# Third layer of a four-layer image kernel: token statistics of the mixers from their modes, synthesis blocks summed straight from PSUM, a part of the last stage on Pool

## The chip, the cores and the metric

The kernel runs on one core of a Trainium2 chip. The metric is the device time of one execution in microseconds (us); the time before is the median of three runs. The engines carry their names in the profile: PE (TensorE, the matmuls), PEld (its weight loads), DVE (VectorE), ACT (ScalarE), POOL (GpSimd, called Pool here) and SP (SyncE, which issues most DMAs). Matmuls write to PSUM, from which DVE and ACT read; all other tiles lie in SBUF.

## The reference

Four layers, each a residual step `x = x + layer(groupnorm(x))`, act on `x` of shape [4, 64, 64, 128]: a selective scan, a Fourier layer with feed-forward, an operator attention, and a 7x7 neighbourhood attention. The third layer is the one that changes. It reads `x` as [images, tokens, height, width]: 64 tokens an image, each a plane of 64x128. Its tail, cut to what matters here:

```python
attn = fno_layer(attn, proj_w, proj_skip_w, proj_skip_b, (H, W))
attn = instance_norm(attn + tokens, attn_norm_g, attn_norm_b)
m = instance_norm(attn, norm2_g, norm2_b)
m = fno_layer(m, mixer_w1, ..., norm=(mixer_norm_g1, mixer_norm_b1), act=_gelu)
m = fno_layer(m, mixer_w2, ..., norm=(mixer_norm_g2, mixer_norm_b2))
out = instance_norm(m, mixer_out_g, mixer_out_b) + attn

def fno_layer(x, spec_w, skip_w, skip_b, out_shape, norm=None, act=None):
    xs = conv1x1(x, skip_w, skip_b)          # a scale and a shift here
    xf = spectral_conv(x, spec_w, out_shape) # 32 x 17 modes of the 2D transform, times weights, back
    if norm is not None:
        xf = instance_norm(xf, *norm)        # mean and variance of each token's plane
    y = xf + xs
    return act(y) if act is not None else y
```

A mixer is thus: transform a plane, multiply the low modes by weights, transform back to `xf`, normalize `xf` by its mean and variance over the plane, add the scaled input. All is float32.

## The kernel before, in words

The layers run one after the other on the one core, from about 0 to 5750 us, to 6220, from 6227 to 7208, and to the end. The third layer keeps an image as a tile of 128 partitions by 32 rows by 128 elements (2 MB): a token's plane lies over the 64 partitions of one half and the 128 elements, two tokens to a row, so `m[:, j, :]` belongs to two tokens and a token's mean and variance are a [128, 32] tile with one column for each `j`. `C4` names four chunks of eight `j`.

`layer2_image` (from L1190) is a generator for one image. `Pace.in_turn` (L1163) runs two of them together, images 0 and 1 and then 2 and 3, and always goes on with the one whose next work starts earliest by a table of costs per engine (`spend`, L1129); with `nc.aside` a piece of work does not move its generator's time. The order that comes out is the order of the instructions on PE, ACT, DVE and Pool (`manual_schedule`); SyncE's queue is ordered by the scheduler. All instructions of this layer are recorded through `Pace`, so the profile puts them on one line, L1155, and they are told apart by their tiles. Each engine takes its instructions in this order, so an instruction that waits holds all behind it.

The parts that matter, for a pair of images:

- **`dft_y`** (L1266): eight groups of four matmuls `pu<-an,z` (or `m`), each copied by ACT into `U`.
- **`spectral`** (L1607): after `dft_y`, four quarters of `pq<-U,quad` (PE) times the weights `mix` on DVE into `Zp`, 68 partitions by 64 tokens by 32 modes. Then `synthesis` (L1283): for each of four `g0`, two matmul groups `pa` copied by ACT to `S`, then two blocks `pb` (u = 0 and 1; each four `j`, 128x512). Each block is copied by ACT to the image tile `sp`, and DVE takes `bn_stats` of each of its four rows.
- **`token_stats`** (L1213): small matmuls `in_pm` that add these statistics over the partitions of a token, with a DVE part `in_d` between.
- After the first mixer: the norm's scale `q1` and shift `f1` (ACT square root, small DVE operations); `sp` is scaled and shifted, in chunks 0 and 2 by ACT (`affine`) and in 1 and 3 by DVE, added to `m`, and ACT takes Gelu of each chunk of `m` (L1663).
- After the second: `m = sp*q2 + m`, 32 DVE operations an image, with `bn_stats` (L1688), then `q3`, `f3`, and the last stage: `m*q3+f3` on ACT, `+z` on DVE, chunk 3 all on DVE, and a DMA for each chunk to the output (L1699).
- Beside the first mixer Pool computes **`residual`** (L1642), `z = z*sa + za + xr`, three operations of 128x1024 for each of the four chunks, where `xr` is the image of `x` loaded again; beside the second, **`grown`** (L1678), `m = m*scal(10)`, four operations. They are called from `copied` (L1627), one step after each block; a step of `residual` is two chunks, one of `grown` is one.

Tiles of 2 MB come from the pool `big`, seven buffers in use in turn: `xg`, `ti`, `z`, `U2`, `sp`, `m`, `xr` of both images share them, so a load waits until the buffer's last reader is done. `S` has three buffers, the PSUM tags `a` and `b` three banks each; `held` gives two more for `in_pm`.

The fourth layer starts from the third's output in DRAM: its loads `x<-x` follow the last output DMAs on SyncE.

Of the kernel before, what the change touches and what calls it, by code (L numbers as in the profile page):

```python
# [11 lines left out]
F32 = mybir.dt.float32  # L12
AF = mybir.ActivationFunctionType
# [4 lines left out]
P = 128  # L18
# [986 lines left out]
def layer2_weights(sh, A, wp, setup, ps, wt, w):  # L1005
# [18 lines left out]
    for n in (1, 2):  # L1024
        load(f"mix{n}", [Q, 32], A[f"mix{n}"])
    pa, pb, vra, vrb, via, vib = (load(name, [Q, 32, 16], A[name], setup) for name in ("pa", "pb", "vra", "vrb", "via", "vib"))
# [22 lines left out]
    for n in (1, 2):  # L1049
        m = w[f"mix{n}"]  # L1050
        nc.vector.tensor_scalar(m, m, qc[:, 0:1], None, ALU.mult)
# [138 lines left out]
def layer2_image(sh, w, pools, x_in, x_out, scr, wt, parity, beside):  # L1190
# [75 lines left out]
    def dft_y(src, scale=None, then=None):  # L1266

        U = large("U2", [P, 2, 32, 64])
        for g in range(NJ // 4):
# [5 lines left out]
            if scale is None:  # L1275
                nc.scalar.copy(Ug, pg)
            else:
                nc.scalar.activation(Ug, pg, AF.Copy, scale=scale)
                then(g)
# [327 lines left out]
    def spectral(src, mix, beside=()):  # L1607
        beside = iter(beside)
        U = yield from dft_y(src)
        Zm = own([Q, 64, 32], "Zp", tmp)  # L1610
        for g in range(4):
            px = ps.tile([Q, 32, 16], F32, name="pq", tag="b")
            for q in range(2):
                nc.tensor.matmul(
                    px, lhsT=w["quad"][:, q, :], rhs=U[:, q, :, 16 * g : 16 * g + 16], start=(q == 0), stop=(q == 1)
                )
            tt(
                Zm[:, 16 * g : 16 * g + 16, :],
                px.rearrange("p r t -> p t r"),
                mix.unsqueeze(1).to_broadcast([Q, 16, 32]),  # L1620
                ALU.mult,
            )
            yield g == 3
        sp = large("sp")
        st = own([P, NJ, 6], "in_st")

        def copied(u, g0, p):  # L1627
            nc.scalar.copy(at(sp, u, g0), p)
            counted(st, sp, block(u, g0))
            nc.aside = True  # L1630
            next(beside, None)
            nc.aside = False

        yield from synthesis(Zm, copied)
        return sp, st


    m = large("m")
    for c in range(4):
        by_rows(m, z, A2, c, ALU.mult)  # L1640
    yield False
    def residual():  # L1642
        xr = large("xr")
        load_image(nc, xr, x_in)
        for n, c in enumerate(C4):
# [3 lines left out]
            if n % 2:  # L1649
                yield  # L1650

    sp, st = yield from spectral(z, w["mix1"], residual())
    mu, var = yield from token_stats(sp, st)
# [9 lines left out]
    for c in range(5):  # L1663
        if c < 4:
            if c % 2:
                by_rows(m, m, f1, c, ALU.add)
                by_rows(sp, sp, q1, c, ALU.mult)
            else:
                affine(sp, sp, q1, f1, c)
            mc = m[:, C4[c], :]  # L1670
            tt(mc, mc, sp[:, C4[c], :], ALU.add)
        if c > 0:
            mc = m[:, C4[c - 1], :]
            nc.scalar.activation(mc, mc, AF.Gelu)
        yield c == 4


    def grown():  # L1678
        for n, c in enumerate(C4):
            nc.gpsimd.tensor_scalar(m[:, c, :], m[:, c, :], scal(10), None, ALU.mult)  # L1680
            yield

    sp, st = yield from spectral(m, w["mix2"], grown())
    mu, var = yield from token_stats(sp, st)
# [3 lines left out]
    for n in range(4):  # L1688
        js = range(8 * n, 8 * n + 8)
        for j in js:  # L1690
            stt(m[:, j, :], sp[:, j, :], q2[:, j : j + 1], m[:, j, :], ALU.mult, ALU.add)
        counted(st, m, js)
        yield n == 3
# [4 lines left out]
    yield True  # L1698
    for n, c in enumerate(C4):  # L1699
        rows = slice(1024 * n, 1024 * n + 1024)  # L1700
# [482 lines left out]
```

## Time and profile before

| what | us |
|---|---|
| median of three runs | 7777.08 (7775.43 to 7779.66) |
| the profiled execution, its own time | 7781.59 |
| its span in the profile | 7779.7 |
| busy in the span: PE, DVE, ACT, POOL | 6337.0, 6747.1, 6112.9, 5675.9 |
| third layer | 6227 to 7208 |
| tail of its first pair (from the first mixer's transform) | 6520 to 6723 |
| tail of its second pair | 7006 to 7208 |
| last `bn_stats` of the first pair's sum ends | 6702.06 |
| DVE's last operation of the first and second pair ends | 6722.5, 7207.6 |
| first load `x<-x` of the fourth layer issued | 7211.14 |

The profiled execution is 4.5 us above the median. The mean granted TensorE clock over the span is 0.964 of full speed. In the page's rows of 40 slices each digit is the busy share of a slice in tenths (9 is 90% or more). A row of the timeline has the start, the length, the engine, the line, the operation, the tiles (out<-in) with partitions x elements, a count, and in brackets how long the engine had been idle and what released it. A row of a group has busy time and mean ns of one after the bar, and then the idle time before them.

### The profile page before, as it was taken

What the parts mean: (1) busy time and instruction counts of PE and PEld (TensorE: products, weight loads), DVE (VectorE), ACT (ScalarE), POOL (GpSimd) and SP (SyncE); (2) the same over time, 40 slices, a digit from 0 to 9 for tenths busy, and PEclk for the clock granted to TensorE, in tenths of its full rate; (3) what the DMA queues carried; (4) which work ended last, traced back from release to release, by engine and by line L of the source; (5) the groups of instructions that cost most, each with busy time, mean ns of one, the idle gap of its engine ahead of it and who ended that gap; (6) DMA issues with size and microseconds to landing.
All of it is one profiled execution on the core that took longest, in us unless ns stands there. A gap on an engine that the chain in (4) does not pass through costs nothing. (4 is left out here: it accounts for less than half of the span.)

```text
span 7779.7 us, 141035 instructions
## 1 busy us (share of the span) xinstructions
PE 6337.0 (81%) x52796; PEld 3998.2 (51%) x52796; DVE 6747.1 (87%) x8097; ACT 6112.9 (79%) x9715; POOL 5675.9 (73%) x2590
## 2 busy tenths in 40 slices
PE   7888888878889877888887777787779968687789
PEld 3544444444455444445554444444457756564566
DVE  7999999999999999999999999999966646556678
ACT  7999999989999998999999999999843323314667
POOL 4989999988999998999999999999930023223233
PEclk8999999999999999999999999999999978788899
DMA  6555556545565554555655445455532142231332
GB/s 171 173 163 175 174 173 176 170 169 165 186 183 179 185 177 162 163 177 179 180 184 180 168 156 185 160 188 177 181 107 63 43 128 61 71 108 40 103 95 81
DMA packets 1325855, 1158.87 MB, mean 149 GB/s; under 512 B 694133, under 2 KB 1119697, under 8 KB 1258226
## 3 DMA queue, kind: packets, MB, share of 16 engines
q1 hardware_dynamic: 1323010, 1148.47, 48.0%
q8 instruction: 416, 6.82, 0.4%
q14 instruction: 269, 2.20, 0.1%
q10 hardware_dynamic: 2160, 1.38, 0.1%
HBM read 956.37 MB, written 189.21 MB: 147 GB/s over the span
## 5 line engine op out<-in xcount | busy, mean ns | idle before, releaser
L688 DVE TENSOR_TENSOR_SCAN h<-dA,state,dB 128x512 f32<-128x512 f32 x4096 | 4921.0, 1266 | 204.4 <-POOL dB L682 79.5
L682 POOL TENSOR_TENSOR dB<-du,Bb 128x1024 f32<-128x1024 f32 x2048 | 4811.7, 2385 | 342.9 <-DVE h L688 208.6
L538 PE MATMUL pt<-ident,h 128*128 128x128 f32 x16384 | 2221.0, 279 | 875.7 <-ACT hT L548 860.0
L687 ACT ACTIVATE dA<-delta,A_neg 128x512 f32<-128x512 f32 x4096 | 2761.1, 697 | 157.6 <-DVE h L688 129.7
L538 PEld LDWEIGHTS pt<-ident,h 128*128 128x128 f32 x16384 | 1807.0, 142 | 1926.3 <-ACT hT L548 1704.7
L548 ACT COPY hT<-pt 128x1024 f32<-128x1024 f32 x2048 | 2080.2, 1016 | 164.7 <-PE pt L538 146.4
L573 PE MATMUL yT<-hT,W 128*32 128x256 f32 x16384 | 1379.6, 409 | 0.4
L573 PEld LDWEIGHTS yT<-hT,W 128*32 128x32 f32 x16384 | 456.0, 150 | 342.5 <-issue 330.9
L161 PE MATMUL cv<-xn,taps 128*128 128x512 f32 x936 | 527.0, 644 | 2.8 <-DVE delta L474 2.8
L1155 POOL TENSOR_TENSOR xg<-xg,so 128x1024 f32<-128x1024 f32 x16 | 39.3, 2466 | 636.5 <-PE pu L1155 613.6
L1900 POOL TENSOR_TENSOR S<-S,sm 128x784 f32<-128x784 f32 x128 | 191.1, 1493 | 419.1 <-DVE sm L1898 256.3
L477 POOL TENSOR_TENSOR du<-delta,u 128x1024 f32<-128x1024 f32 x128 | 304.3, 2377 | 79.0 <-DVE delta L474 78.9
L465 PE MATMUL dp<-xd,w_dt 65*128 65x512 f32 x512 | 288.8, 646 | 69.9 <-ACT Ct L456 47.0
L448 PE MATMUL xd_ps<-u,w_x 128*48 128x512 f32 x512 | 251.8, 615 | 23.6 <-DVE e L360 18.1
L1907 ACT ACTIVATE S<-S,mx 128x196 f32<-128x196 f32 x512 | 227.8, 448 | 35.9 <-DVE mx L1934 35.4
L161 PEld LDWEIGHTS cv<-xn,taps 128*128 128x128 f32 x936 | 139.2, 188 | 180.5 <-issue 160.4
L914 ACT ACTIVATE h<-pf,b 128x512 f32<-128x512 f32 x128 | 87.7, 687 | 117.2 <-PE pf L913 99.2
L474 DVE SCALAR_TENSOR_TENSOR delta<-delta,dp 128x512 f32<-128x512 f32 x256 | 170.6, 667 | 4.3 <-ACT delta L471 1.0
L1862 PE MATMUL pt<-ident,S 128*98 128x128 f32 x1024 | 166.3, 287 | 3.5 <-POOL S L1900 2.0
L465 PEld LDWEIGHTS dp<-xd,w_dt 65*128 65x128 f32 x512 | 76.5, 188 | 174.5 <-ACT Ct L456 99.9
L1155 POOL TENSOR_TENSOR WX<-wr,Xs 128x544 f32<-128x544 f32 x40 | 58.0, 1449 | 148.2 <-issue 61.8
L471 ACT ACTIVATE delta<-delta 128x512 f32<-128x512 f32 x256 | 165.9, 649 | 0.0
(378 smaller groups left out, 7030.6 us busy)
## 6 DMA issues: line engine op xcount, KB each, us to landing
Bb<-l_B SPq DMA_DIRECT2D x512, 1024.0 KB
W<-l_W SPq DMA_DIRECT2D x512, 256.0 KB
l_y<-y SPq DMA_DIRECT2D x127, 512.0 KB
u<-l_xr SPq DMA_DIRECT2D x64, 512.0 KB
u<-l_xw SPq DMA_DIRECT2D x64, 512.0 KB
y<-l_y SPq DMA_DIRECT2D x56, 512.0 KB
V<-l_v SPq DMA_DIRECT2D x512, 49.0 KB
y<-l_y SPq DMA_DIRECT2D x80, 256.0 KB
```

The costliest lines, as they stand in the source:

```text
L161: nc.tensor.matmul(pm, lhsT=taps[:, s, t, :], rhs=xn[:, dy : dy + 8, dx : dx + 64], start=(t == 0), stop=(t == 8),)
L448: nc.tensor.matmul(bank["x"], lhsT=w_x[:, s, k, :], rhs=u[:, s, :], start=(s == 0), stop=(s == 1))
L465: nc.tensor.matmul(bank[s], lhsT=w_dt[:, k, s * P : (s + 1) * P], rhs=xd, start=True, stop=True)
L477: nc.gpsimd.tensor_tensor(du, delta, u, ALU.mult)
L538: nc.tensor.transpose(pt[:, j, s, :], G["h"][:, s, t0 : t0 + 32, :].rearrange("p t n -> p (t n)"), sh.ident)
L548: return lambda: nc.scalar.copy(hT, pt.rearrange("p j s d -> p j (s d)"))
L573: nc.tensor.matmul(U["yT"][e][32 * jo : 32 * jo + 32, qo % 2, :], lhsT=U["Ws"][G["g"]][:, :, 4 * q + j], rhs=hT[:, j, :], start=((e, jo) n ...
L682: nc.gpsimd.tensor_tensor(dB, du, B_now[:, q : q + 1, :].to_broadcast([P, 2, CH]), ALU.mult)
L687: nc.scalar.activation(dA, delta[:, s, :], AF.Exp, scale=A_neg[:, k, s, n : n + 1])
L688: nc.vector.tensor_tensor_scan(h[:, s, :, q], dA, dB[:, s, :], state[:, s, n : n + 1], ALU.mult, ALU.add)
L1900: nc.gpsimd.tensor_tensor(Sv, Sv, U["sm"].unsqueeze(2).to_broadcast([P, 4, 196]), ALU.mult)
L1907: nc.scalar.activation(Sn, Sn, AF.Exp, bias=U["mx"][:, n : n + 1], accum_out=sm[:, n : n + 1])
```

## The change: what it does

The mixers no longer write the synthesized plane to `sp`. In `spectral`, after each quarter's product `Zp = pq*mix`, a matmul `pn` with a constant matrix `power` (34 x 512) forms sums of the modes' real and imaginary parts, ACT squares it to `sq`, and DVE reduces it over the modes (`tensor_reduce` of modes 1 to 31, `tensor_copy` of mode 0) into `total`. Three small matmuls for each half of the partitions then give a token's mean (from its zeroth mode) and variance (from the sums of squares) in `pm`. For this the weights `mix` are formed in the weights' setup with two more constants (`mir`, `once`), loaded by four more small DMAs.

Because mean and variance are known before the synthesis, `q1` and `f1` are too: `m += f1` by eight rows at a time on DVE, and each block `pb` goes straight from PSUM into the sum, `m = pb*q1 + m` (DVE, one operation for each `j`), with Gelu of a chunk after its last block. `residual` is called from there. In the second mixer the blocks with u = 0 are summed in the same way; those with u = 1 are scaled by ACT into a tile `qs` and added by DVE in one operation; `bn_stats` of the sum follows. `grown` is called from the groups of the second mixer's `dft_y`. In the last stage chunk 0 is computed by Pool (three operations), chunks 1 and 2 as before, chunk 3 on DVE as before.

```diff
--- before
+++ after
@@ layer2_weights
         load(f"mix{n}", [Q, 32], A[f"mix{n}"])
+        load(f"mir{n}", [Q, 32], A[f"mir{n}"], setup)
+    load("power", [Q, 226], A["c_power"])
+    once = load("once", [Q, 32], A["c_once"], setup)
...
-        nc.vector.tensor_scalar(m, m, qc[:, 0:1], None, ALU.mult)
+        nc.vector.scalar_tensor_tensor(m, m, qc[:, 0:1], once, ALU.mult, ALU.mult)
+        nc.vector.scalar_tensor_tensor(m, w[f"mir{n}"], qc[:, 7:8], m, ALU.mult, ALU.add)
@@ layer2_image
-    def spectral(src, mix, beside=()):
-        beside = iter(beside)
-        U = yield from dft_y(src)
+    def spectral(src, mix, then=None):
+        U = yield from dft_y(src, None, then)
         Zm = own([Q, 64, 32], "Zp", tmp)
+        total = own([P, NJ, 6], "in_st")[0:34].rearrange("p j k -> p (j k)")[:, 0:128].rearrange("p (n t) -> p n t", n=2)
         for g in range(4):
+            part = slice(16 * g, 16 * g + 16)
             px = ps.tile([Q, 32, 16], F32, name="pq", tag="b")
             for q in range(2):
+                nc.tensor.matmul(px, lhsT=w["quad"][:, q, :], rhs=U[:, q, :, part], start=(q == 0), stop=(q == 1))
+            tt(Zm[:, part, :], px.rearrange("p r t -> p t r"), mix.unsqueeze(1).to_broadcast([Q, 16, 32]), ALU.mult)
+            yield False
+            pn = ps.tile([34, 16, 32], F32, name="pn", tag="a")
+            nc.tensor.matmul(pn, lhsT=w["power"][:, 0:34], rhs=Zm[:, part, :], start=True, stop=True)
+            sq = tmp.tile([34, 16, 32], F32, name="sq", tag="S2", bufs=3)
+            nc.scalar.activation(sq, pn, AF.Square)
+            nc.vector.tensor_reduce(total[:, 0, part], sq[:, :, 1:32], AX.X, ALU.add)
+            nc.vector.tensor_copy(total[:, 1, part], sq[:, :, 0])
+            yield g == 3
+        pm = held([P, 2, NJ], "in_pm")
+        for u in range(2):
+            half = slice(64 * u, 64 * u + 64)
+            nc.tensor.matmul(pm[half, 0, :], lhsT=w["power"][:, 162:226], rhs=Zm[:, u:64:2, 0], start=True, stop=True)
+            for n in range(2):
                 nc.tensor.matmul(
+                    pm[half, 1, :],
+                    lhsT=w["power"][0:34, 34 + 64 * n : 98 + 64 * n],
+                    rhs=total[:, n, u:64:2],
...
-        sp = large("sp")
-        st = own([P, NJ, 6], "in_st")
-        def copied(u, g0, p):
-            nc.scalar.copy(at(sp, u, g0), p)
-            counted(st, sp, block(u, g0))
...
-    for c in range(5):
-        if c < 4:
-            if c % 2:
-                by_rows(m, m, f1, c, ALU.add)
-                by_rows(sp, sp, q1, c, ALU.mult)
-            else:
-                affine(sp, sp, q1, f1, c)
-            mc = m[:, C4[c], :]
-            tt(mc, mc, sp[:, C4[c], :], ALU.add)
...
+    for c in range(4):
+        if c in (0, 1, 2, 3):
+            by_rows(m, m, f1, c, ALU.add)
...
+    def mixed(u, g0, p):
+        for n, j in enumerate(block(u, g0)):
+            stt(m[:, j, :], p[:, n, :], q1[:, j : j + 1], m[:, j, :], ALU.mult, ALU.add)
+        if u == 1:
+            mc = m[:, C4[g0 // 4], :]
             nc.scalar.activation(mc, mc, AF.Gelu)
+            if (0, 0, 0, 0)[g0 // 4] == 0:
+                aside(rest)
+    yield from synthesis(Zm, mixed)
+    def grown(g):
+        if g % 2:
+            nc.aside = True
+            mc = m[:, C4[g // 2], :]
+            nc.gpsimd.tensor_scalar(mc, mc, scal(10), None, ALU.mult)
+            nc.aside = False
+    Zm, mu, var = yield from spectral(m, w["mix2"], grown)
...
+    def summed(u, g0, p):
+        if u in (1,):
+            t = tmp.tile([P, 4, DM], F32, name="qs", tag="S2", bufs=3)
+            for n, j in enumerate(block(u, g0)):
+                nc.scalar.activation(t[:, n, :], p[:, n, :], AF.Copy, scale=q2[:, j : j + 1])
+            tt(at(m, u, g0), at(m, u, g0), t, ALU.add)
+        for n, j in enumerate(block(u, g0) if u not in (1,) else ()):
+            stt(m[:, j, :], p[:, n, :], q2[:, j : j + 1], m[:, j, :], ALU.mult, ALU.add)
+        counted(st, m, block(u, g0))
...
+    for n in (0,):
+        c = C4[n]
+        nc.aside = True
+        for v, op in ((wide(q3, c), ALU.mult), (wide(f3, c), ALU.add), (z[:, c, :], ALU.add)):
+            nc.gpsimd.tensor_tensor(m[:, c, :], m[:, c, :], v, op)
+        nc.aside = False
+        put(n)
     for n, c in enumerate(C4):
+        if n in (0,):
+            continue
+        if n in (3,):
```

## The prediction

> **What bounds the kernel now.** I read the page's head first, then the table of busy time by stage, then the groups and waits of the stage that the diff touches, then its timeline. From the page, the span and the rows of busy tenths and clock tenths:
>
> ```profile
> span 7779.7 us, 141035 instructions
> PE   7888888878889877888887777787779968687789
> DVE  7999999999999999999999999999966646556678
> ACT  7999999989999998999999999999843323314667
> POOL 4989999988999998999999999999930023223233
> PEclk8999999999999999999999999999999978788899
> ```
>
> Each digit is 194.5 us. Up to digit 29 VectorE is full (the scan). The third layer is digits 33 to 37: there no engine is full. It runs from 6227 to 7208 us, and the diff touches the tail of each of its two pairs of images: 6520 to 6723 and 7006 to 7208. The table of stretches for the first tail, its last row the whole (start and end, length, busy time of PE, weight loads, DVE, ACT and POOL with counts, granted clock, DMA share, GB/s):
>
> ```profile
> 6520.00:6557.00 37.00, 37.00 (x187) 23.66 (x188) 21.18 (x33) 14.75 (x26) 19.38 (x9) 1.00 0.22 57
> 6557.00:6591.00 34.00, 22.30 (x102) 13.19 (x98) 19.75 (x62) 15.48 (x31) 31.18 (x16) 0.86 0.25 63
> 6591.00:6633.00 42.00, 28.51 (x140) 22.63 (x142) 21.80 (x25) 27.45 (x50) 18.37 (x6) 0.75 0.00 0
> 6633.00:6671.00 38.00, 37.52 (x162) 20.63 (x158) 23.10 (x99) 18.31 (x32) 5.68 (x2) 1.00 0.22 56
> 6671.00:6702.00 31.00, 5.76 (x26) 5.19 (x24) 28.34 (x116) 10.62 (x28) 0.00 (x0) 0.54 0.44 119
> 6520.00:6723.00 203.00, 136.66 (x635) 90.36 (x634) 126.47 (x360) 96.24 (x190) 74.61 (x32) 0.80 0.23 60
> ```
>
> PE is full twice (at 1.00, around the two transforms), the sum (6671 to 6702) is DVE's. Of 203 us PE works 136.66 and DVE 126.47: what counts is who waits for whom. Three groups (busy time and mean ns, then idle time before them and what ended it) and one wait (total us, times, longest) of the tail, which the change takes out:
>
> ```profile
> L1155 DVE BATCH_NORM_STATS2 in_st<-sp 128x6 f32<-128x128 f32 x128 | 26.2, 276 | 34.8 <-ACT sp L1155 34.8
> L1155 DVE SCALAR_TENSOR_TENSOR m<-sp,q,m 128x128 f32<-128x128 f32 x64 | 17.4, 341 | 0.2
> L1155 ACT COPY sp<-pb 128x512 f32<-128x512 f32 x32 | 17.3, 589 | 21.0 <-PE pb L1155 21.0
> PE in_pm L1155 <- DVE in_st L1155: 30.5, 6, 19.5
> ```
>
> PE waits 30.5 us for statistics that DVE takes of sp. Last, what happens where Pool works beside DVE, and what stops Pool:
>
> ```profile
> 6522.50 2.92 DVE L1155 TENSOR_TENSOR m<-z,A 128x1024 f32<-128x1024 f32 x1
> 6542.81 2.35 POOL L1155 TENSOR_TENSOR z<-z,xr 128x1024 f32<-128x1024 f32 x1 [15.64 <-DMA xr<-x]
> 6581.10 1.98 DVE L1155 TENSOR_TENSOR in_d<-in_d 128x64 f32<-128x64 f32 x1
> 6610.24 7.27 PE L1155 MATMUL pu<-an,m 128*128 128x128 f32 x40 [11.47 <-ACT U L1155]
> ```
>
> The product m<-z,A takes 1.21 us alone and 2.92 beside a Pool operation: it seems to stand still for most of one. A small product takes 0.2 alone (in_d<-in_st,in_pm 0.23, just before it) and 1.98 here. Pool stops 15.64 us for a load. The last row is a transform after 11.47 us of idle PE: five groups of eight matmul passes, 1.45 us each, where a group at full clock is 0.89; rival B comes back to it.
>
> **The change, part by part (one pair).** *Counts.* DVE loses 128 statistics on sp (26.2), 64 sums from SBUF (17.4), 8 m+sp (9.8), 4 products sp*q (4.9); it gains 96 sums from PSUM, 4 more m+f (4.6), 8 adds of 128x512 (0.7 each), 16 reductions (bound by the 128x512 row 0.69), 16 small copies (0.1 to 0.16). ACT loses 32 copies sp (17.3), 32 affines (12.7), 16 of the 48 last affines (6); it gains 16 squares (0.58) and 32 scaled copies (0.31). PE gains 16 products of 512 columns (0.86, half a pq pair of 1.72) and 4 groups of small ones (1.3). It loses the small products of sp's statistics (5). Net: DVE -10, ACT -17, PE +13.5. *A sum from PSUM* has no row. Bounds: 0.26 (from one start to the next in the 64 sums from SBUF) and 0.34 (that row's mean length, nothing overlapped). I take 0.27, since z<-z,pb from PSUM takes 0.676 and an SBUF product of that size 0.69.
>
> [...]
>
> *The order, walked* with the durations above, first pair, us from the start of the span.
> 1. **m=z*A2.** The first image's load of x (xr) waited on SyncE for the first mixer's last pq; with sp's buffer gone it stands behind the weight loads (wr) and waits for neither PE nor ACT, so Pool goes on at 6527.2. Each of the four products left then stands beside a Pool operation (2.35, 1.89, 1.90, 2.35, together +8.4): the end 6532.7 becomes 6541.1. Bounds 0 and +8.5.
> 2. **Statistics from the modes.** The first pn starts at 6541.9; in PE's new order there lie, to the first image's pm, 6 pn (5.2), 6 pq (10.3), 2 transform groups (1.8) and pm (1.3): 18.6, so 6560.5. Then the seven small DVE operations that took 7.7 before (6579.2 to 6586.9), with a product from pq, a reduction and a copy between: 9.7, first f1 at 6570.2.
> 3. **m+=f1**, eight by 1.14, and the second image's scales 1.8: 6581.1 undisturbed. The second image's xr still waits for the first image's last pq (6556 by the same order) and lands 4.4 later (before: issued 6538.45, Pool on at 6542.81), so half of Pool's 24 operations stand from 6560 on; five here hold one of DVE's each (2.05 on average): +10.3, 6591.4. The weight loads behind xr in SyncE's queue are not needed before the next pair.
> 4. **Synthesis into m, with Gelu.** PE has 29.2 for both images (8 quarters of 3.65), 6 done by then (three PSUM banks): 23 left. DVE's 64 sums (17.3) and ACT's 17 lie beside; the S copies stand behind the Gelus (8 by 1.05) in ACT's order, of which I let 5 show. So 28, to 6619.4; last Gelu 6620.9 (6619.1 before).
> 5. **Second transform.** In the new order two of the first image's groups stand among the last blocks; eleven more (9.8) begin when PE is through with its last block, 6618.5, just ahead of DVE's last sums: 6628.3. Before, PE idled 11.47 and began cold, and the last group came at 6644.8; now three groups are left, inside step 6. This is where the walk gains.
> 6. **Statistics again**, 1.7+0.9 and a PE chain of 22.7: first synthesis at 6653.6. m*scal, on Pool, lies beside it: 8 operations by 2.8 (5.68 for two in the stretch from 6633), done by 6648 and needed by the first sums about 6656: no cost; without that cover one or two of them, 2.8 to 5.6.
> 7. **Sum.** Eight quarters. PE 3.85 (pa 1.92, pb 1.92), DVE 4x0.27+8x0.195+0.7=3.3, ACT 2.3: PE's, 30.8, and statistics, tail 6.2: 37, to 6690.6 (6702.06 before).
> 8. **Last stage.** Before 20.4. The first chunks on Pool (1.9+1.9+2.35 an image, 12.3 with the second image's f3 some 4 later) end ahead of DVE's last, so the puts that stand behind theirs on SyncE, and the next loads of x, lose nothing. But they hold one additional operation of DVE: 22.4; bounds 20 (none) and 25.4 (two and a half by 2). End 6713.0 instead of 6722.5.
>
> Saving 9.5 a pair, 19 both. The second pair follows the same path (its stretches agree within 4 us). It passes on whole: the fourth layer's PE waits 23.46 us for the load x<-x, which SyncE issues after the last put. *Setup*: 4 small loads, and 4 operations on 68x32 in place of 2 (0.23 each), in a stretch where PE is busy 186.7 of 200: price 0, at most 2.
>
> The sum is made against the profiled run: 7781.59 (span 7779.7), which is 4.5 over the median 7777.08. So 7781.6-19=7762.6, and against the median **7758**. The measurement tells 0.2% (15.6 us) from no change.
>
> **Rivals.** *A, Pool doesn't stand in DVE's way.* Then steps 1 to 3 lose their holds: 8.4, 10.3, and some 6 of the small operations (four by 1.5), 24.6 together; with the 9.5 that is 34 a pair, **7709**. For it: the statistics of sp beside the same Pool rows keep their 1.64 for eight. Against: 2.92 beside 1.21, 1.98 beside 0.22.
> *B, slower: PE at half clock in steps 4 and 5.* Before step 4 PE is done with its statistics by 6573, fills three PSUM banks and idles until DVE's sums start (6591); then its blocks wait for S copies behind Gelus. The profile has this case, ten microseconds in which ACT feeds PE between Gelus:
>
> ```profile
> 6590.00:6600.00 10.00, 5.75 (x24) 5.27 (x24) 7.08 (x11) 9.97 (x22) 3.26 (x1) 0.57 0.00 0
> ```
>
> At 0.57 (7.08 and 9.97 there: DVE and ACT are the busy ones) the 23+9.8 us of PE work in steps 4 and 5 take 57.5, and the 5 of waits vanish in it: +20, net +10 a pair, **7797**; at the 0.50 of the same view's 6604 to 6610, +28, 7814. It decides from 13 us of that work at 0.57 on (+9.8). Against: once PE was fed in the row of 7.27 above, the next groups were at 0.89 again, and the stretch after it shows 1.00.
> *C, no measurable difference.* The two images cover each other before, so the removed work lay beside other work, and the gain is spent: last stage 25.4 (+3), step 4 begun cold (+2), copies (+0.5). 4 a pair: **7769**.
>
> **How the numbers follow.** Forecast 0.47, A 0.15, B 0.18, C 0.20. The forecast's own range, from the bounds of steps 1, 8 and the PSUM sums (0.09 by 96 is 8.6 a pair, half of it beside PE's work), is 7742 to 7772; the part of it above 7761.5, within 0.2%, is a fifth. Faster: A's 0.15 and 0.39 of the forecast's, 0.54. Slower: B's 0.18 and 0.02 of C, whose spent gain may be overspent, 0.20. Within: 0.08 and 0.18, 0.26. The range goes from 7705, under A, to 7800, over B's first case: out of it are B's colder half (0.1) and what is faster than A (0.05).
>
> **What would show it.** In the profile after: m<-z,A products at 2 to 3 us beside Pool, ending near 6541 (step 1); f1 near 6570, no DVE wait for sp; PE's granted clock in 6580 to 6620 (B); the last transform group near 6628; last statistics near 6690; the first xr without a wait. A sum from PSUM far over 0.27, Pool's 24 operations stretched, or a transform still at 0.75 of the clock would make me wrong.

## The result, and the profile after

The kernel after takes **7801.0 us** (median of nine, 7797.3 to 7805.2), the kernel before on the same chip 7777.6 (median of nine, 7774.3 to 7785.0): a ratio of 1.0031, 95% interval 1.0022 to 1.0039. It is 23 us slower, where 7758 and a gain were forecast. The profiled execution of after took 7800.54, 19.0 more than that of before, and it is this one that the rows explain. From the page, the same rows as of before:

```profile
span 7798.7 us, 141011 instructions
...
PE   7888888878889877888887777787789878788789
...
DVE  7999999999999999999999999999966556556678
ACT  7999999999999998999999999999842322313567
POOL 4989999988999999999999999999920023324233
PEclk8999999999999999999999999999999988888899
```

Outside digits 33 to 37 little is different, and within them no engine is full. Over the span ACT is busy for 38 us less (6112.9 to 6075.1; -34 was counted), but DVE for 26 more (6747.1 to 6773.1) where 20 less was counted, and PE and Pool for 61 and 41 more. Nearly all of it is in the third layer: the fourth layer's first load is issued 19.6 us later (7230.73 for 7211.14). Of that, 1.3 are there when the third layer starts, 2.1 and 3.4 come in the stretches ahead of the two tails, where both kernels do nearly the same work, and the rest in the two tails themselves: measured from the first product m<-z,A to the end they are **5.0 and 8.1** longer, where the prediction had them 9.5 shorter each. The first tail in the table of stretches (start and end, length, busy time of PE, weight loads, DVE, ACT and POOL with counts, granted clock, DMA share, GB/s), and below it two stretches within the second and third:

```profile
6520.00:6557.00 37.00, 26.21 (x142) 17.61 (x141) 30.02 (x32) 10.43 (x19) 28.34 (x11) 0.84 0.00 1
6557.00:6591.00 34.00, 28.43 (x83) 13.70 (x82) 27.71 (x35) 7.63 (x13) 24.70 (x10) 0.75 0.24 62
6591.00:6633.00 42.00, 38.84 (x145) 22.90 (x146) 21.33 (x68) 16.93 (x25) 6.54 (x3) 0.84 0.01 1
6633.00:6671.00 38.00, 37.13 (x169) 19.13 (x168) 13.68 (x26) 14.32 (x24) 22.18 (x9) 1.00 0.43 111
6671.00:6706.00 35.00, 31.43 (x127) 16.86 (x126) 27.87 (x109) 16.69 (x48) 0.00 (x0) 0.95 0.00 1
6706.00:6731.00 25.00, 5.36 (x24) 4.83 (x24) 20.21 (x32) 12.80 (x33) 12.29 (x6) 0.50 0.48 146
...
6573.00:6589.00 16.00, 13.25 (x36) 8.41 (x37) 15.76 (x15) 3.94 (x6) 15.69 (x7) 0.50 0.00 0
6596.00:6610.00 14.00, 14.00 (x30) 7.73 (x29) 4.58 (x15) 5.30 (x8) 0.00 (x0) 0.51 0.01 1
```

Three things to see. In the first stretch DVE is busy for 30.02 us, where it was for 21.18 before, with fewer instructions, while Pool is busy for 28.34: they stand in each other's way. In the two lower rows PE works for 13.25 of 16 us and for 14.00 of 14, and is granted 0.50 and 0.51 of its clock. And the tail's last 25 us (6706 to 6731), in which PE works 5.36, are longer than the 20.4 of before. Now three groups of this tail (busy time and mean ns, then the idle time before them):

```profile
L1159 DVE SCALAR_TENSOR_TENSOR m<-pb,q,m 128x128 f32<-128x128 f32 x96 | 26.3, 343 | 28.0 <-PE pb L1159 20.6 <-issue 7.2
...
L1159 DVE TENSOR_TENSOR m<-z,A 128x1024 f32<-128x1024 f32 x8 | 20.3, 2602 | 0.0
...
L1159 DVE TENSOR_TENSOR m<-m,f 128x1024 f32<-128x1024 f32 x10 | 15.4, 1570 | 0.1
```

A sum from PSUM takes 343 ns (341 from sp before), as the prediction took it. The product m<-z,A takes 2602 ns in the mean, 1638 before. The timeline of DVE, POOL and PE shows why, and where PE stands:

```profile
6523.59 20.26 DVE L1159 TENSOR_TENSOR m<-z,A 128x1024 f32<-128x1024 f32 x8
6524.95 2.75 POOL L1159 TENSOR_TENSOR z<-z,sa 128x1024 f32<-128x1024 f32 x1 [49.33 <-PE pu L1159]
...
6577.43 7.19 PE L1159 MATMUL pa<-sy,Zp 68*128 68x256 f32 x16
...
6583.60 1.83 DVE L1159 TENSOR_TENSOR q<-q,A 128x32 f32<-128x32 f32 x1
...
6587.33 6.77 DVE L1159 TENSOR_TENSOR m<-m,f 128x1024 f32<-128x1024 f32 x4
6594.02 2.15 DVE L1159 SCALAR_TENSOR_TENSOR m<-pb,q,m 128x128 f32<-128x128 f32 x8
6595.28 2.64 PE L1159 MATMUL pb<-S,bd 64*128 64x512 f32 x4 [2.47 <-DVE m L1159]
6597.85 7.20 PE L1159 MATMUL pa<-sy,Zp 68*128 68x256 f32 x16
...
6674.99 1.13 DVE L1159 SCALAR_TENSOR_TENSOR m<-pb,q,m 128x128 f32<-128x128 f32 x4 [7.24 <-issue]
```

Eight products take 20.26 (12.56 before; 9.16 undisturbed, in e2 below), each of Pool's operations beside them 2.75 to 3.21 where the same ones take 1.90 and 2.35 a little later: both take longer. A product of 128x32 takes 1.83 where its like take 0.19. Sixteen `pa` take 7.2 us, where eight take 1.99 in the second mixer. Pool's wait of 15.64 us for `xr` is gone: the load is issued at 6477.4 instead of 6538.5, since sp's buffer is free.

### The profile page after: what moved, and what is told of

Same layout as the page of the kernel before. It is cut to its first block, busy times and chain, and to the rows that moved or that the text cites. A ratio compares the mean times of both kernels' runs of the same rounds, so it can differ in the third digit from the quotient of the medians.

```text
span 7798.7 us, 141011 instructions
## 1 busy us (share of the span) xinstructions
PE 6397.7 (82%) x52860; PEld 4010.2 (51%) x52860; DVE 6773.1 (87%) x7951; ACT 6075.1 (78%) x9651; POOL 5716.8 (73%) x2602
```

## The experiments

The time of each, with the kernel before on the same chip; "tails" are the two, first product to end (before: 202.3 and 201.5; after: 207.3 and 209.6).

| kernel | median us | before | ratio (95%) | tails |
|---|---|---|---|---|
| after | 7800.99 | 7777.58 | 1.0031 (1.0022 to 1.0039) | 207.3, 209.6 |
| e1: last stage as before | 7797.70 | 7774.15 | 1.0030 (1.0019 to 1.0041) | 211.1, 210.9 |
| e2: residual later | 7746.71 | 7774.15 | 0.9966 (0.9953 to 0.9979) | 180.8, 189.6 |
| e3: PE fed | 7792.53 | 7774.15 | 1.0025 (1.0015 to 1.0035) | 210.2, 214.7 |
| e4: e1 and e2 | 7742.30 | 7774.15 | 0.9958 (0.9941 to 0.9974) | 184.9, 184.7 |
| e5: PE fed longer | 7796.81 | 7774.61 | 1.0030 (1.0019 to 1.0042) | 205.7, 215.1 |
| e6: xr loaded as late as before | 7778.04 | 7774.61 | 1.0006 (0.9996 to 1.0015) | 202.8, 200.0 |
| e7: e2, PE fed | 7755.83 | 7774.61 | 0.9977 (0.9967 to 0.9986) | 184.4, 189.9 |
| e8: PE fed, right places in both pairs | 7789.10 | 7777.02 | 1.0017 (1.0008 to 1.0026) | 203.1, 203.4 |
| e9: e2, PE fed, both pairs | 7749.33 | 7777.02 | 0.9963 (0.9948 to 0.9978) | 185.0, 180.8 |
| e10: images staggered | 7829.40 | 7777.02 | 1.0063 (1.0046 to 1.0080) | 220.9, 221.8 |
| e11: before, residual later | 7834.50 | 7777.02 | 1.0072 (1.0057 to 1.0087) | 225.9, 228.8 |
| e12: e2, still later | 7746.70 | 7778.97 | 0.9961 (0.9947 to 0.9974) | 180.8, 185.4 |

The kernels ran on several chips, on which the kernel before differs by up to 5 us. So differences between two of them are counted below from each one's own before: after is 23 us over it, e2 27 under it, 51 apart. The tails are those of the one profiled execution of each kernel.

**e1: is it the part of the last stage on Pool?** That part goes back to ACT and DVE.

```diff
-    for n in (0,):
+    for n in ():
...
-        if n in (0,):
-            continue
```

> The changed kernel with the last stage of the kernel before: chunk 0 is scaled by ACT and added by DVE again, nothing of that stage on Pool. Theory 'Pool stands in the way of the last stage': from the last statistics to DVE's last operation takes 25.3 us in the changed kernel and took 20.4 before; it goes back to 20.4 to 21.5, the small operations q3, f3 and in_d to 0.2 each, so 4 to 5 us a pair, 8 to 10 in all, a median near 7792. Rival 'ACT bounds the stage': 48 affines of 0.39 are 18.6 us in place of 12.4, and what Pool's part costs DVE comes back on ACT; then the stage stays within 2 us and the median between 7797 and 7803.

The last stage takes 24.5 and 25.0 us, where it took 25.2 and 25.7 in after, and the time doesn't tell the two kernels apart. Pool's part is not the cause. What is longer in the last stage shows in the timeline of before, around the first pair's last sums, against the same stage of after. First before:

```profile
6683.52 9.34 ACT L1155 ACTIVATE m<-m,f,q 128x128 f32<-128x128 f32 x24 [0.40 <-DVE f L1155]
...
6687.72 1.21 DVE L1155 TENSOR_TENSOR m<-m,z 128x1024 f32<-128x1024 f32 x1
...
6697.28 1.20 DVE L1155 TENSOR_TENSOR m<-m,z 128x1024 f32<-128x1024 f32 x1
```

Then after:

```profile
6690.26 0.64 PE L1159 MATMUL in_pm<-in_st,tok 128*128 128x32 f32 x4
...
6698.41 0.22 DVE L1159 TENSOR_TENSOR in_d<-in_st,in_pm 128x64 f32<-128x64 f32 x1
...
6705.64 0.34 DVE L1159 RECIPROCAL q<-q 128x32 f32<-128x32 f32 x1
...
6711.58 2.25 DVE L1159 TENSOR_TENSOR m<-m,z 128x1024 f32<-128x1024 f32 x1 [1.20 <-ACT m L1159]
...
6719.69 3.37 DVE L1159 TENSOR_TENSOR m<-m,z 128x1024 f32<-128x1024 f32 x2 [3.31 <-ACT m L1159]
...
6729.69 1.22 DVE L1159 TENSOR_TENSOR m<-m,f 128x1024 f32<-128x1024 f32 x1
```

Before, ACT scales the first image's chunks from 6683.5 and DVE adds them between the second image's last sums, which end at 6702. So only one image's last stage is left for the 20.4 us behind the last statistics. After, the statistics of one image are complete at 6690.3, where PE adds them up, 15 us ahead of the other's (6705.7). But in DVE's order the steps from there to its q3 and f3 stand behind the other image's sums (`in_d` at 6698.4, q at 6705.6). So the last stages of both stand behind all sums, one by one.

**e2: Pool's residual moved to where DVE sums from PSUM.** The residual's factor is read from a copy of `sa`, which DVE makes behind the image's m+=f1; so Pool can't start earlier.

```diff
-            for v, op in ((wide(sa), ALU.mult), (wide(za), ALU.add), (xr[:, c, :], ALU.add)):
+            for v, op in ((wide(vs), ALU.mult), (wide(za), ALU.add), (xr[:, c, :], ALU.add)):
...
+    nc.nc.vector.tensor_copy(vs, sa)
     def mixed(u, g0, p):
```

> The changed kernel, but Pool's residual takes its factor from a copy of sa (in the tile vs) that DVE makes after m+=f1, so its 24 operations of a pair start some 45 us later, beside the sums into m and the second transform. Theory 'Pool stands in DVE's way in the first half': the eight products m<-z,A go from 20.3 us to about 10, the small copies of 1.3 to 2.3 to 0.2, the eight m+f of 18 us to about 11, and the sums from PSUM keep 2.16 for eight beside Pool; the sums start 18 to 22 us earlier, 36 to 44 in all, a median of 7757 to 7765. Rival 'the hold only moves': the sums, which read m from SBUF too, are held by up to 24 operations of about 2, step 4 grows by as much, and the median stays at 7795 to 7805. Rival 'PE is the path there anyway': under 10 us in all.

7746.7: 27 us less than before and 51 less than after, more than was expected. The sums into m start 22.0 and 23.9 us earlier in the two tails. From its timeline:

```profile
6518.99 9.16 DVE L1159 TENSOR_TENSOR m<-z,A 128x1024 f32<-128x1024 f32 x8
...
6562.30 4.05 DVE L1159 TENSOR_TENSOR m<-m,f 128x1024 f32<-128x1024 f32 x2
6562.53 2.74 POOL L1159 TENSOR_TENSOR z<-z,vs 128x1024 f32<-128x1024 f32 x1 [91.52 <-DVE vs L1683]
...
6567.40 2.16 DVE L1159 SCALAR_TENSOR_TENSOR m<-pb,q,m 128x128 f32<-128x128 f32 x8 [1.05 <-PE pb L1159]
...
6589.34 2.16 DVE L1159 SCALAR_TENSOR_TENSOR m<-pb,q,m 128x128 f32<-128x128 f32 x8 [2.71 <-PE pb L1159]
```

The products take 9.16, and the first f1 is there 34.7 us after their start, where it was there after 50.7. The sums from PSUM, all beside Pool here, keep 2.16 for eight. Of the m+=f1 only the three that are left when the first image's residual begins stand beside Pool (4.05 for two, another at 2.15; two take 2.35 undisturbed).

In these rows eight products, which read two tiles from SBUF, take 20.26 us beside Pool and 9.16 without it, and eight sums from PSUM 2.16 beside Pool and 2.15 without it (after, at 6594).

**e6: only the load undone.** The first image's and the second's `xr` get their buffer early, but their load waits for ACT's last copy of `U`.

```diff
     def spectral(src, mix, then=None):
         U = yield from dft_y(src, None, then)
+        if then is None:
+            nc.nc.scalar.copy(xr[:, 0, 0:1], U[:, 0, 0, 0:1])
...
     def residual():
-        xr = large("xr")
         load_image(nc, xr, x_in)
...
+    xr = large("xr")
     rest = residual()
```

> The changed kernel, with the first image's load of xr held back as in the kernel before: ACT writes one column of xr behind the last copy into U, and the load waits for that, so Pool stops after two operations until some 20 us into the tail. Theory 'the load that the change lets go early makes the first hold': the eight m<-z,A take 12.6 us again (20.3 in the changed kernel), the first Zp comes 7.7 us earlier; but Pool's other 22 operations (45 us) come later by as much and hold the small operations and m+=f to the end of that stage, so the sums into m start only 2 to 8 us earlier; 4 to 14 in all, a median of 7787 to 7797. Rival 'all holds are the early load's': as the late residual, under 7765.

7778.0, no different from before (0.9996 to 1.0015): 20 us less than after, more than expected. From its timeline:

```profile
6519.58 12.57 DVE L1159 TENSOR_TENSOR m<-z,A 128x1024 f32<-128x1024 f32 x8
...
6531.95 2.40 POOL L1159 TENSOR_TENSOR z<-z,xr 128x1024 f32<-128x1024 f32 x1 [5.42 <-DMA xr<-x]
```

Pool waits for the load again, and the products take what they took before (12.56). The tails are 4.6 and 9.7 shorter than after's; the rest of the 20 lies elsewhere, in work that is the same in both kernels. That rest isn't explained: over all kernels here the stretches ahead of the tails differ by up to 5.5 us from one profiled execution to the next.

**e11: the control.** e2's edit in the kernel before: `vs` is copied behind f1, and the residual is called from the loop that adds f1 and sp.

```diff
-            for v, op in ((wide(sa), ALU.mult), (wide(za), ALU.add), (xr[:, c, :], ALU.add)):
+            for v, op in ((wide(vs), ALU.mult), (wide(za), ALU.add), (xr[:, c, :], ALU.add)):
...
-    sp, st = yield from spectral(z, w["mix1"], residual())
+    sp, st = yield from spectral(z, w["mix1"])
...
+    nc.nc.vector.tensor_copy(vs, sa)
+    rest = residual()
     for c in range(5):
+        nc.aside = True
+        next(rest, None)
+        nc.aside = False
```

> The control: the kernel before with the late residual (its factor from a copy of sa made behind f1, the rest as it was). Theory 'the late residual's 50 us belong to the changed kernel': before, Pool stopped 15.6 us for the load of its own accord, one of eight products was held (1.7) and some five small operations (1.2 each); so 3 to 6 us a pair at most, and m*scal and the sums behind may give part of it back: a ratio of 0.9985 to 1.0005. Rival 'any kernel of this layer gains from it as much': 0.9965 or less, as the changed kernel with the late residual.

7834.5, **57 us slower** than before, against both expectations. Its timeline:

```profile
6520.20 9.17 DVE L1155 TENSOR_TENSOR m<-z,A 128x1024 f32<-128x1024 f32 x8
...
6586.71 3.37 DVE L1155 TENSOR_TENSOR m<-m,f 128x1024 f32<-128x1024 f32 x1
...
6590.00 2.91 DVE L1155 TENSOR_TENSOR sp<-sp,q 128x1024 f32<-128x1024 f32 x1
6592.95 2.80 DVE L1155 TENSOR_TENSOR m<-m,sp 128x1024 f32<-128x1024 f32 x1
```

The products are free here too (9.17), but Pool now stands beside m+f, sp*q and m+sp, which read two tiles from SBUF; most of them take 2.8 to 3.4 instead of 1.2. DVE works without a gap from 6584.5 on, and the last m+sp ends at 6637.8, where it ended at 6613.6 in before: 24 us, as much as this tail is longer. The same move has opposite signs in the two kernels. So what counts is not that Pool works later, but which DVE operations it works beside: a place beside sums from PSUM exists only in the changed kernel.

**e12: later still.** In e2's kernel the copy stands behind the first eight sums from PSUM, so no m+=f1 should be held.

```diff
-    nc.nc.vector.tensor_copy(vs, sa)
...
     def mixed(u, g0, p):
...
+        if u == 1 and g0 == 0:
+            nc.nc.vector.tensor_copy(vs, sa)
```

> The late residual once more, its factor copied behind an image's first eight sums from PSUM in place of ahead of them, so that none of the eight products m+=f stands beside Pool (with the copy ahead, two took 4.05 together and one 2.15, alone 1.14 each). Theory 'Pool holds DVE operations that read two tensors from SBUF and not those that read PSUM': no m<-m,f over 1.25, the sums keep 2.16 for eight beside Pool, the sums into m start 2 to 3 us earlier, a ratio to the kernel before of 0.9955 to 0.9963 (0.9966 with the copy ahead). Rival: the wait for PE's blocks takes up what is saved, ratio 0.9963 to 0.9972.

```profile
6560.97 4.62 DVE L1159 TENSOR_TENSOR m<-m,f 128x1024 f32<-128x1024 f32 x4
...
6579.40 2.16 DVE L1159 SCALAR_TENSOR_TENSOR m<-pb,q,m 128x128 f32<-128x128 f32 x8 [4.70 <-PE pb L1159]
```

In this timeline the holds are gone (4.62 for four), and DVE waits for PE's blocks instead (4.70 here). The time isn't different from e2's (0.9961 for 0.9966): from here on, DVE's sums wait for PE.

**e3, e5 and e8: is it the half clock in step 4?** Idle matmuls, 128x128 into an unused part of a PSUM tile, are put into PE's order so that it stays busy until DVE's sums begin: before the last `pn`, before `pm` and before a `pb` of the images' syntheses. They are not counted in the order's table of costs. In e3 (8, 20 and 10 of them):

```diff
+    def warm(pm, n):
+        nc.aside = True
+        for _ in range(n):
+            nc.nc.tensor.matmul(pm[:, 2:6, :].rearrange("p a j -> p (a j)"), lhsT=w["an"], rhs=w["an"], start=True, stop=True)
+        nc.aside = False
...
+            if g == 3:
+                pm = held([P, 6, NJ], "in_pm")
+                if then is None and parity == 0:
+                    warm(pm, 8)
...
+        if then is None and parity == 0:
+            warm(pm, 20)
...
-    yield from synthesis(Zm, mixed)
+    yield from synthesis(Zm, mixed, (lambda: warm(pm, 10)) if parity == 1 else None)
```

> The changed kernel with 38 matmuls of 128x128 a pair that write an unused part of the tile of in_pm and are read by nobody: 8 before the last pn and 20 before the last statistics of the second image, 10 before the fourth block, where PE stood idle 1.9, 3.7 and 2.5 us. The order of all other work is unchanged. Theory 'half clock in step 4': the clock stays near 1.00 from 6573 to 6611 where it was 0.50 for 28 of 38 us, DVE's wait of 9.4 us for pb falls to about 2, and a pair gets 5 to 8 us shorter, 10 to 16 in all, a median near 7788. Rival 'the S copies behind the Gelus make the wait': no change at a full clock, 7799 to 7803, or 2 to 4 slower by the added matmuls.

This one doesn't decide. The clock was 1.00 from 6560 to 6588, but then the ten matmuls were through before DVE's sums, PE idled 5.65 us and was at 0.50 again; and in the second pair the buffers by which the places were picked belong to the images the other way round, so the matmuls stood in wrong places. In e5 there are 34 in the third place:

```diff
-    yield from synthesis(Zm, mixed, (lambda: warm(pm, 10)) if parity == 1 else None)
+    yield from synthesis(Zm, mixed, (lambda: warm(pm, 34)) if parity == 1 else None)
```

> As the kernel that feeds PE before (added matmuls of 128x128 that nobody reads), with 34 in place of 10 ahead of the fourth block, since there PE still stood idle 5.65 us and its clock was 0.50 for the 12 us behind that. Theory 'a short idle puts step 4 at half clock': no row of 0.50 between 6560 and 6615, DVE's wait of 9.1 us for pb falls to 2 to 3.5, the sums into m take 29 us and not 36; the pair's tail (first m<-z,A to DVE's last) is 199 to 203 us against 207.3 and 209.6 in the changed kernel, the median 10 to 16 under the changed kernel's 7801. Rival 'PE waits for S behind the Gelus': the 9.1 us stay at full clock, the tail stays at 206 to 210.

The first pair now does what was meant; in the table of stretches, against 0.50 and 0.51 of after:

```profile
6568.00:6583.00 15.00, 15.00 (x88) 11.07 (x88) 14.76 (x15) 3.83 (x6) 14.69 (x7) 1.00 0.01 1
...
6590.00:6604.00 14.00, 13.03 (x49) 7.16 (x49) 7.62 (x26) 7.13 (x11) 0.00 (x0) 1.00 0.01 2
```

The sums into m take 30.9 us, 5.4 less than in after (36.3), but 3.1 are lost again in the second mixer, and the first tail is 1.6 shorter. In the second pair the matmuls are on the path (7.86 us of them at 7100), and the whole is no faster than after. e8 puts them by the images' order, so in the right places in both pairs:

```diff
+    ahead = len(beside) == 1
...
+                if fill is not None and g0 == 12 and e == 2:
+                    fill(0)
...
+                if fill is not None and g0 == 4 and u == 1:
+                    fill(34)
...
-                if then is None and parity == 0:
+                if then is None and not ahead:
```

> The changed kernel with the added matmuls at the same three places in both pairs. In the two runs before, the places were picked by the buffer number, which the images of the second pair have the other way round, so there the matmuls stood elsewhere and partly on the path; in the first pair 8, 20 and 34 held the clock at 1.00 throughout and the sums into m took 30.9 us against 36.3. Now the same is expected in the second pair: 71 to 102 us after the first m<-z,A in place of 71 to 110. Theory of the half clock: the sums into m end 5 to 8 us earlier in each pair, 10 to 15 in all at that point; if nothing behind gives it back, the median is 7786 to 7792. Rival 'it is given back behind' (in the first pair of the run before, 3 of the 5 were lost again by the second mixer): 7793 to 7799.

7789.1, 12 us over before where after is 23 over it: 11 less than after. The sums take 32.9 in both pairs, where they took 36.3 and 39.1, and the tails are 4.2 and 6.2 shorter (in the profiled execution, the fastest of e8's ten). So the half clock is a real cause, worth some 10 us of the two tails; it may be more, since the idle matmuls are work of their own and the half clock wasn't taken away wholly. The table of stretches has:

```profile
6574.00:6581.00 7.00, 7.00 (x20) 3.75 (x18) 6.86 (x6) 3.73 (x6) 6.84 (x4) 0.58 0.00 0
```

Here the clock falls with PE busy for 7.00 of 7.00 us.

**e7 and e9: the half clock once the residual is late.** In e2's kernel, idle matmuls as in e3 (4, 6 and 10; e7), or as in e8 with a fourth place, before a late `pa` (4, 6, 7 and 8; e9). e7 against e3:

```diff
-                    warm(pm, 8)
+                    warm(pm, 4)
...
-            warm(pm, 20)
+            warm(pm, 6)
```

> The late residual together with added matmuls where PE then stood idle (4, 6 and 10). With the late residual the clock was 0.50 from 6555 to 6567 and DVE waited 1.05 and 3.0 us for blocks in the first pair, 9 in the second. Theory of the half clock: those waits go to under 1 each, 2 to 4 us in the first pair, 3 to 6 in the second, a median 4 to 10 under that of the late residual (7746.7 against a kernel before at 7774.2), a ratio to before of 0.9953 to 0.9961. Rival: no difference beyond 0.1%, or slower by up to 2 a pair if the added work gets in the way.

And e9 against e8, besides the same two:

```diff
-                    fill(0)
+                    fill(8)
...
-                    fill(34)
+                    fill(7)
```

> The late residual with 4, 6, 7 and 8 added matmuls at the places where PE stands idle in it, in both pairs alike (the last 8 ahead of the block column whose copy S stands behind a Gelu). Theory of the half clock: no stretch at 0.50 from the statistics to the end of the sums into m, these sums take 28 to 31 us in both pairs (31.9 and 35.9 with the late residual alone), and the time is 4 to 10 us under that kernel's, a ratio to before of 0.9953 to 0.9961 (late residual alone: 0.9966). Rival: the added work stands in the way, ratio 0.997 or more.

Neither gives the gain that was expected: e7's median is 9 us over e2's, though the intervals overlap, and e9 (ratio 0.9963) isn't different from it (0.9966). In e9's second pair the clock is 1.00 throughout the stage, and the sums still take 33.0 (e2: 31.9 and 35.9). In e7 the clock was 1.00 until 6577 and 0.50 from there to 6584. There PE waited, as its timeline shows, for a copy `S`, which stands in ACT's order behind the Gelus:

```profile
6577.49 2.08 PE L1159 MATMUL pa<-sy,Zp 68*128 68x256 f32 x4 [2.46 <-ACT S L1159]
```

With the residual out of the way PE waits for none of DVE's sums in the first pair of e2 from 6556 to 6600 (2.47 us in after) and 1.02 for a copy `S`, and the idle matmuls find little to fill.

**e10: the images staggered**, to have one image's last stage between the other's sums again: the second synthesis of one is ordered after all sums of the other.

```diff
+    ahead = len(beside) == 1
...
+    if not ahead:
+        yield lambda: len(beside) > 3
     yield from synthesis(Zm, summed)
+    beside.append(None)
```

> The changed kernel, but in the second mixer the first image of a pair starts its synthesis only when the other image's sums are issued: PE's and DVE's order puts one image's blocks, statistics and first add of the last stage ahead of the other's. Theory 'the last stage lost its cover': in the kernel before the first image's last stage lay inside the second image's sums, in the changed kernel both images end together; from the last statistics to DVE's last operation it takes 25.2 and 25.7 us, and here 21 to 23; 4 to 9 us in all, if the sums do not get longer. Rival: the stage stays within 1 us of 25, or the sums get longer by as much, and the median stays at 7796 to 7803.

```profile
6697.31 1.06 PE L1159 MATMUL in_pm<-in_st,tok 128*128 128x32 f32 x4 [3.53 <-DVE in_st L1159]
...
6710.13 1.12 DVE L1159 SCALAR_TENSOR_TENSOR m<-pb,q,m 128x128 f32<-128x128 f32 x4 [10.37 <-PE pb L1159]
```

The last stage takes 19.4 us in both pairs (25.2 and 25.7 in after), so its cause is the lost cover, as read above. That both images end together, as was expected here of the changed kernel, doesn't hold: their sums lie one behind the other in after too, and it is the steps behind one image's statistics that come late. But the last statistics come at 201.5 and 202.4 us of the tails instead of 182.1 and 183.9: as the timeline shows, PE waits for one image's statistics ahead of the other's blocks, and DVE waits 10.37 for a block. It is 29 us slower than after.

**e4: e1 and e2 together.**

```diff
-            for v, op in ((wide(sa), ALU.mult), (wide(za), ALU.add), (xr[:, c, :], ALU.add)):
+            for v, op in ((wide(vs), ALU.mult), (wide(za), ALU.add), (xr[:, c, :], ALU.add)):
...
+    nc.nc.vector.tensor_copy(vs, sa)
...
-    for n in (0,):
+    for n in ():
...
-        if n in (0,):
-            continue
```

> Both edits, the late residual and the last stage of the kernel before. If both theories hold and they are independent: 44 to 54 us under the changed kernel, a median of 7747 to 7757, below the kernel before. If the hold only moves: 7787 to 7795.

7742.3, the lowest median of all: 0.9958 of before (0.9941 to 0.9974). It is faster than before and after; from e2 its interval doesn't tell it apart.

## Why the prediction was wrong, step by step

The times are those of the first pair from the first product on, the second pair's in brackets; the predicted ones from the same point, which the prediction put at 6520.2.

| step | predicted, length | measured |
|---|---|---|
| 1: m=z*A2 | 20.9 | 20.3 (20.3) |
| 2: first f1 | 29.1 | 30.4 (31.0) |
| 3: m+=f1, to the first sum | 21.2 | 19.7 (19.7) |
| 4: synthesis and sums into m | 28 | **36.3 (39.1)** |
| 5 to 7: second mixer, to the last statistics | 71.2 | 75.4 (73.7) |
| 8: last stage | 22.4 | **25.2 (25.7)** |
| sum | 192.8 | 207.3 (209.6) |

**Steps 1 to 3 were right**, in mechanism and within 1.5 us each in size: the load stands early, four products are held (20.3 for 20.9), and the operations around m+=f1 are held by about as much as was priced. In the second image's rows, m+=f1 is held by 3.6 and the small operations ahead of it by 4.9 and 1.2, 9.7 for the 10.3 that the step put on m+=f1 alone.

**Step 4 is the term that failed**: 28 us, with 5 of waits, became 36.3 and 39.1. Its PE work was priced at full clock. What it met was rival B's case: 0.50 in 6573 to 6589 and again in 6596 to 6610. The first sets in as PE falls idle for 2.83 us, shortly behind an idle time of 1.91, the second just behind one of 2.47. The argument that the prediction set against B, that the transforms were at full clock again soon after PE was fed (the row of 7.27, in which three groups take 1.7 to 1.9 and only the last two 0.9; 1.45 is a mean of both), does not carry over to `pa` and `pb`: with these PE worked for 13 to 15 us without a gap and stayed at 0.50. e5 and e8 show it by giving the time back, 5.4 in the first pair and 3.4 and 6.2 of the sums in the two. At full clock they still take 30.9 (e5, first pair), so some 3 us over the 28 aren't shown to be the clock's; what they are stays open. B's own price was too high (20 over the forecast a pair, where the term grew by 8.3 and 11.1), since step 5 lost nothing: from the last sum into m to the first `pq` of the second mixer the prediction had 8.9, and 8.9 it was. So it is partly luck that B's 7797 lies near the measured 7801: the steps behind and the stretches ahead of the tails made up for it.

**Steps 6 and 7** took 4.2 more in the first pair and 2.5 in the second. From the first `pq` of the second mixer to its first `pa` it is 27.1 in both, where step 6 had 25.3; why is open. From that `pa` to DVE's first sum it is 8.7 in the first pair, where the clock is 0.76 in 6668 to 6675, and 7.1 in the second, where it is 1.00; in e5's first pair DVE is idle for 10.35 ahead of that sum, where it is for 7.24 in after. So some 1.6 of the 4.2 are the half clock again, in a smaller place. This was read from the traces and not tried alone.

**Step 8** lies at its upper bound, 25.4, but for another reason than given. Not Pool's part holds it (e1), but the cover that one image's last stage had among the other's sums is gone (before's and after's rows above, e10). Rival C had this price; the prediction's question, what hides the work and what it costs if that cover is gone, was asked for Pool's part and not for the stage itself.

In the first pair these (8.3, 4.2 and 2.8, less 0.8 in steps 1 to 3) are the whole 14.5 between a tail 9.5 shorter and one 5.0 longer; in the second they are 16.8 of 17.6, and before's second tail was 0.8 shorter than the first, from which the walk set out. So of the 43 us between the forecast and the median the tails are 32; 7 lie ahead of the tails, and 4 are the difference between the two profiled executions (19.0) and the medians (23.4). The 5.5 us in the stretches ahead of the tails stay open; they are within what these stretches differ by from one execution to the next, and the setup, priced at 0 and at most 2, can't be told apart there.

**PSUM** sums were right at 0.27 each: 2.15 us for eight, 26.3 for the 96. `m*scal` on Pool was hidden, as priced: in the first pair it ends at 6655.3, and the first sum begins at 6675.0.

**Rival A** ("Pool doesn't stand in DVE's way") was wrong in what it said and near in its price: it put the holds at 24.6 a pair, 49 in all, and in e2, which moves Pool to where it holds almost nothing, the sums into m start 22.0 and 23.9 earlier, and the whole is 51 faster than after. With the residual so moved the change is 27 us faster than before; with only the load as late as before (e6) it isn't different from before. So the early load, which nobody would look for in "statistics from the modes", takes some 20 of the 23 us. The prediction saw the load and charged it in full; the sign of the tails then hung on step 4, without whose 8.3 and 11.1 they would be some 3 us shorter than before each.

## What to carry to other kernels

A change that frees a buffer moves the loads that wait for it, and with them whatever works on what they bring (here `xr` was issued at 6477.4 instead of 6538.5, and eight products took 20.26 us instead of 12.56): ask which operations it will then stand beside. In these kernels Pool's large operations belong beside DVE's sums from PSUM (2.16 us for eight, 2.15 without Pool), not beside operations that read two tiles from SBUF (20.26 for eight, 9.16 without Pool); this choice alone was 51 us one way and, in the kernel before, which has no such sums, 57 the other. Price PE's work behind an idle time at the clock that the nearest row of the same matmuls shows, not at that of another shape (here 0.50 and 0.51 for `pa` and `pb`, where `pu` was at 1.00 after some 6 us).

## What was not expected of the hardware

- The half clock lasts, with mostly `pa` and `pb` (68 and 64 rows of contraction), for 13 to 15 us of PE without a gap (after: 0.50 in 6573 to 6589, 0.51 in 6596 to 6610), while under `pu` (128 rows) it was over 5 us into the row of 7.27, in the trace of before: 0.50 up to 6615, 0.70 in 6615 to 6616, 1.00 from there. That it is the number of rows that matters was not tried.
- The clock also falls with PE busy throughout (e8, 0.58 in 7.00 us), where by the kernel's order the matmuls turn from 128 rows to `pa` (20 of them in 6570 to 6572, 9 in 6574 to 6576); so idle time alone doesn't bring it about. The same turn kept 1.00 in e3 (6560 to 6588) and in e5 (6568 to 6583), so it isn't the turn alone either.
- When DVE and Pool meet in such operations, both lose: 20.26 us for eight products in place of 9.16 on DVE, 2.75 to 3.21 for one operation in place of 1.90 to 2.35 on Pool. Small ones lose most in proportion: a 128x32 product 1.83 for 0.19, a copy of 34x16 up to 2.31 for 0.16, so sixteen of these copies take 9.4 us in after and 4.7 in e2.
